# Moving the next block's queries between scores and values, and a block's first sums of exponentials by up to a unit, in a four-layer kernel on one core

## The chip, the cores and the metric

The kernel runs on one core of one Trainium2 chip. The metric is the device time of one execution in microseconds (us). The core has five engines that run side by side, each through its own instructions in order: PE (TensorE, products), DVE (VectorE), ACT (ScalarE, which does the exponentials), POOL (GpSimd) and SP (SyncE, which issues transfers). An engine waits for another one through semaphores.

## The reference, cut to what matters

The input `x` has 4 images of 128 channels and 64 x 64 pixels, so 4096 tokens of 128 channels per image. Four layers follow each other, and each adds its result to its input:

```
x = x + attention(group_norm(x))       # layer 0, self-attention over the 4096 tokens of an image
x = x + conv5x5(group_norm(x))         # layer 1
x = x + state_space(group_norm(x))     # layer 2, a scan over the 4096 tokens, both directions
x = x + conv3x3(group_norm(x))         # layer 3
```

The change lies in layer 0. Its core is

```
q, k, v = xt @ Wq.T + bq, xt @ Wk.T + bk, xt @ Wv.T + bv
attn = softmax((q @ k.T) * 128 ** -0.5)
out = attn @ v
```

## The kernel before, in words

**Images and stages.** An image goes through attention, the 5 x 5 convolution (`conv_pairs`), the preparation of the scan (`scan_prep`, `scan_operands`), the scan itself (`scan_core`) and, later, the last convolution. Layers 0 and 1 and the preparation of image b+1 are generators whose steps are put between the ticks of image b's scan. So image 0's attention stands alone, and the attention of images 1, 2 and 3 runs beside the scan of the image before. A `credit` decides how many steps go between two ticks: each step yields what it costs PE by the author's constants (`PRODUCT`, 0.86). The order of every engine's instructions is thus fixed when the program is built.

**Attention.** The weights of queries and keys are multiplied ahead of time into `wqk`, so the normalised image `xn` serves as keys. An image has 8 blocks of 512 tokens, and a block is worked off in 32 units of 128 keys; `u` counts all 256 units of an image, and `blk, j = divmod(u, 32)`. The pieces that matter:

- `queries(blk)`: a product `pr` of `wqk` and 512 columns of `xn` (L446), into PSUM bank "s"; then ACT copies it with a bias to `r` in SBUF (L448). It was called at `j == 17` for the next block, at the end of the unit.
- `scores(u)`: a product `sc` of 128 columns of `xn` and the block's `r` (L479), into bank "s" for even units and bank "s2" for odd ones; then ACT takes the exponential (L485) into slot `u % 8` of a ring in SBUF, called `exchange` in the profile.
- `values(w)`, two units behind: adds the product of `v` and ring slot `w` to `acc` (L491).
- `sums(w)`: sums of exponentials of four slots, as four products of 32 columns side by side, into `zp` (L513) in bank "z". In image 0 two other engines add them up in place of it (`side_sums`, L530 to L533). In images 1 to 3 a group of four is put on the list `due` with a first unit and a last one. `sums_due`, at the head of each unit, takes it in the first unit in which the scan has put its own products of 32 columns (`y`, L1272) before it, or else in the last one.
- At the end of a block `turn`, `invert`, `widen_out` and `settle` follow in units 1, 2, 4 and 5 after it. They use bank "z" too, and `settle` (L579, L580) is the last to read it, on DVE.

A float32 product of 512 columns is two passes on PE, so two rows in the profile. ACT's queue in images 1 to 3 also holds the scan's decays `da` (L1220) and copies of its last column (`last`, L1253). DVE runs the scan (`da`, `hc`, L1237 and L1240), POOL the products `db` (L1227) and part of the weighting (`hc`, L1258).

The whole program stands twice in the build; the second copy, with row maxima taken off, runs only where the sums leave a safe range.

Of the kernel before, what the change touches and what calls it, by code (L numbers as in the profile page):

```python
# [45 lines left out]
PRODUCT, HOP, SLOT, PACE, ENDPACE, AHEAD = 0.86, 1.7, 0.7, 2.8, 1.5, 4  # L46
# [6 lines left out]
def conv_preact_kernel(  # L53
# [26 lines left out]
    NM = L // MM  # L80
# [13 lines left out]
    def bank(tag, name):  # L94
        return pools.get(tag, ps).tile([P, MM], F32, tag=tag, name=name)
# [205 lines left out]
    NRING = 8  # L301
# [132 lines left out]
    def attention(b, xs, xn, v, st, safe, loads):  # L434
# [6 lines left out]
        def after(u, n, f, *args):  # L441
            later.setdefault(u + n, []).append((f, args))

        def queries(blk):
            pr = bank("s", f"pr_{b}_{blk}")
            nc.tensor.matmul(pr, wqk, xn[:, bass.ts(blk, MM)], start=True, stop=True)  # L446
            rq[blk] = pools["bg"].tile([P, MM], F32, tag="r", name=f"r_{b}_{blk}")
            nc.scalar.activation(rq[blk], pr, AF.Identity, bias=bqk)  # L448

        def row_max(blk):  # L450

            part = small.tile([P, TPM, NM], F32, tag="part", name=f"part_{b}_{blk}")
            for t in range(TPM):
                for k in range(NM):
                    pp = bank("s", f"pmax_{b}_{blk}_{t}_{k}")
                    nc.tensor.matmul(
                        pp, rq[blk][:, bass.ts(t, P)], xn[:, bass.ts(k, MM)],
                        start=True, stop=True,
                    )
                    nc.vector.tensor_reduce(part[:, t, k : k + 1], pp, AX.X, ALU.max)  # L460
            m = small.tile([P, TPM], F32, tag="rmax", name=f"rmax_{b}_{blk}")
            nc.vector.tensor_reduce(m, part, AX.X, ALU.max)
            pb = bank("s", f"pmb_{b}_{blk}")
            spread(pb, m)
            mb[blk] = pools["bg"].tile([P, MM], F32, tag="w", bufs=4, name=f"mb_{b}_{blk}")
            nc.scalar.copy(mb[blk], pb)
# [9 lines left out]
        def scores(u):  # L476
            blk, j = divmod(u, NJT)
            sc = bank(("s", "s2")[u % 2], f"sc_{b}_{u}")
            nc.tensor.matmul(sc, xn[:, bass.ts(j, P)], rq[blk], start=True, stop=True)  # L479
            pt = ring[:, u % NRING, :]  # L480
            if safe:
                nc.vector.tensor_tensor(pt, sc, mb[blk], ALU.subtract)
                nc.scalar.activation(pt, pt, AF.Exp)
            else:
                nc.scalar.activation(pt, sc, AF.Exp)  # L485

        def values(u):
            blk, j = divmod(u, NJT)
            if j == 0:
                acc[blk] = bank("a", f"acc_{b}_{blk}")  # L490
            nc.tensor.matmul(  # L491
                acc[blk], v[:, j, :], ring[:, u % NRING, :], start=j == 0, stop=j == NJT - 1
            )
# [3 lines left out]
        due = []  # L497

        def sums_due(u):
            beside = "collected" in ready  # L500
            ready.discard("collected")
            if due and due[0][1] <= u and (beside or u >= due[0][2]):
                sums(due.pop(0)[0])
                return PRODUCT
            return 0.0

        def sums(u):

            blk, j = divmod(u, NJT)
            if j == 3:  # L510
                zp[blk] = bank("z", f"zp_{b}_{blk}")
            for g in range(4):
                nc.tensor.matmul(  # L513
                    zp[blk][g * 32 : (g + 1) * 32, :], ones[:, :32],
                    ring[:, (u - 3 + g) % NRING, :], start=j == 3, stop=j == NJT - 1,
                    tile_position=(0, g * 32), skip_group_check=True,
                )
# [7 lines left out]
        def side_sums(u):  # L525
            blk, j = divmod(u, NJT)
            eng, e = (nc.vector, nc.gpsimd)[j % 2], "dp"[j % 2]
            if j < 2:
                sides[blk, e] = fill.tile([P, MM], F32, tag=f"side{e}", name=f"side{e}_{blk}")
                eng.tensor_copy(sides[blk, e], ring[:, u % NRING, :])  # L530
            else:
                s = sides[blk, e]
                eng.tensor_tensor(s, s, ring[:, u % NRING, :], ALU.add)  # L533

        def evict_sums(blk):
            zs = None
            if not fill:
                zs = pools["bg"].tile([P, MM], F32, tag="zs", bufs=1, name=f"zs_{b}_{blk}")
                nc.scalar.copy(zs, zp.pop(blk))
            state[blk] = None, zs  # L540

        def evict(blk):
            raw = pools["bg"].tile([P, MM], F32, tag="raw", bufs=1, name=f"raw_{b}_{blk}")
            nc.scalar.copy(raw, acc.pop(blk))
            state[blk] = raw, state[blk][1]
# [44 lines left out]
        for u in range(N):  # L590
            blk, j = divmod(u, NJT)
            cost = sums_due(u)
            if safe and j == 0:
                row_max(blk)
            scores(u)
            cost += PRODUCT
            w = u - 2
            if w >= 0:
                if w < N - HELD:
                    values(w)  # L600
                    cost += PRODUCT
                d = w % NJT
                if fill:
                    side_sums(w)
                elif d == NJT - 1:
                    sums(w)
                    cost += PRODUCT
                elif d % 4 == 3:
                    due.append((w, u + (2 if d == 3 else 1), u + NRING - 5))
                if d == NJT - 1:  # L610
                    evict_sums(blk - 1)
                    evict(blk - 1)
                    for n, f in ((1, turn), (2, invert), (4, widen_out), (5, settle)):
                        after(u, n, f, blk - 1)
            if j == 17 and blk + 1 < NM:
                queries(blk + 1)
                cost += PRODUCT
            for f, args in later.pop(u, ()):
                f(*args)
                cost += PRODUCT if f in (turn, widen_out) else 0.0  # L620
            next(loads, None)
            yield cost or HOP
        for w in (N - 2, N - 1) if fill else ():
            side_sums(w)
        blk = NM - 1
# [718 lines left out]
    def program(safe):  # L1344
# [24 lines left out]
        def front(b, xn, v):  # L1369

            xs = large(b + 1, f"xs_{b}")[:, :L]
            st = Sums(f"e{b}")
            yield from attention(b, xs, xn, v, st, safe, load(xs, b))
            st2 = Sums(f"s{b}")

            yield from conv_pairs(b, xs, f"A{b % 2}", st, st2, b > 0 or safe)
            if b + 1 == B:
                nc.sync.dma_start(m3, main_w)

            def mat(name):  # L1380
                return dram.tile([NCH, P, CH], F32, tag=name, name=f"{name}_{b}")

            mats4[b] = (
                [mat("bm"), mat("cm")], mat("dd"), mat("dxd"), mat("xcd"),
                dram.tile([P, L], F32, tag="xsd", bufs=B, name=f"xsd_{b}"),
            )
            ynds[b] = dram.tile([NM, P, MM], F32, tag="ynd", bufs=B, name=f"ynd_{b}")
            operands = yield from scan_prep(b, xs, st2, mats4[b])
            if b + 1 < B:
                return (yield from both(operands, start(b + 1, 10)))  # L1390
            yield from operands
            last_weights()
# [215 lines left out]
```

## Time and profile before

| | us |
|---|---|
| median of 3 runs | 4472.4 |
| lowest and highest of them | 4471.19, 4475.15 |
| the profiled execution's own time | 4469.3 |
| its span, first to last instruction | 4467.5 |
| PE busy in it | 3980.8 (89%) |
| DVE busy | 3726.3 (83%) |
| POOL busy | 3638.1 (81%) |
| ACT busy | 2399.7 (54%) |

The clock that PE was granted is 0.942 of full speed in the mean over the span. Scores (L479) take PE 1084.4 us and values (L491) 1048.4, the largest two of its groups; the scan's `y` 654.6, the sums 201.6. A busy time says how full an engine is and not whether it sets the pace; for that one cuts the span into stages and reads, stage by stage, which engine waits for which. In the trace, "idle before" a row, in brackets, names the engine and line that ended the wait. Where two rows of ACT end close together, a wait of PE for the first may be put down to the second (`last` in place of `r`).

### The profile page before, as it was taken

Reading aid. Unit: us, or ns where it says so; the run is one execution under the profiler, and the core shown is the slowest. Engines: PE = TensorE matmul, PEld = TensorE weight load, DVE = VectorE, ACT = ScalarE, POOL = GpSimd, SP = SyncE. Lnnn points to the kernel's source line nnn. Section 1 sums busy time; section 2 is a strip of 40 time slices with the busy share of each in tenths; the row PEclk is TensorE's granted clock in tenths of the full one; section 3 lists DMA queues with packets and bytes.
Section 4 is the critical chain, followed back from the end, with each engine's and each line's share of the span. In section 5 each row is a group of like instructions: output and inputs, shape, how many; then the busy total and the mean of one; then the engine's idle time right before and its main releaser. Section 6 shows DMA issues by size and latency. Waiting matters only on the chain. (4 is left out here: it accounts for less than half of the span.)

```text
span 4467.5 us, 43584 instructions
## 1 busy us (share of the span) xinstructions
PE 3980.8 (89%) x13480; PEld 1470.8 (33%) x13480; DVE 3726.3 (83%) x3703; ACT 2399.7 (54%) x4425; POOL 3638.1 (81%) x1728
## 2 busy tenths in 40 slices
PE   8999997999999979999999989999999758576776
PEld 4444433333333323333333333333333112121222
DVE  4712217999999989999999899999999899999995
ACT  3333217666665476666664576666654744444542
POOL 3433207999999978999999889999999889999995
PEclk9999999999999999999999999999999879787888
DMA  1000016544454565454545565455445666656562
GB/s 63 9 1 1 0 51 227 177 171 169 171 186 158 176 224 202 172 177 172 175 152 171 202 236 177 163 177 179 170 163 177 220 221 204 227 202 230 185 229 79
DMA packets 210002, 719.86 MB, mean 161 GB/s; under 512 B 24800, under 2 KB 25696, under 8 KB 209632
## 3 DMA queue, kind: packets, MB, share of 16 engines
q1 hardware_dynamic: 208160, 716.26, 45.9%
q8 instruction: 108, 1.77, 0.2%
q14 instruction: 134, 1.10, 0.1%
q10 hardware_dynamic: 1600, 0.73, 0.1%
HBM read 649.07 MB, written 67.83 MB: 160 GB/s over the span
## 5 line engine op out<-in xcount | busy, mean ns | idle before, releaser
L1227 POOL TENSOR_TENSOR db<-dx,br 128x1024 f32<-128x1024 f32 x1024 | 2399.9, 2365 | 231.1 <-DMA br<-bm 55.0
L1220 ACT ACTIVATE da<-de,a_neg 128x512 f32<-128x512 f32 (+1 forms) x1796 | 1342.9, 751 | 665.3 <-DVE da L1237 378.0
L479 PE MATMUL sc<-r,x 128*128 128x512 f32 x2048 | 1084.4, 612 | 16.0 <-ACT r L448 11.5
L491 PE MATMUL acc<-exchange,v 128*128 128x512 f32 x2048 | 1048.4, 594 | 1.7
L1258 POOL TENSOR_TENSOR hc<-hc,cr 128x1024 f32<-128x1024 f32 x401 | 947.7, 2363 | 19.3 <-ACT last L1253 16.5
L485 ACT ACTIVATE exchange<-sc 128x512 f32<-128x512 f32 x1024 | 604.7, 591 | 590.5 <-PE sc L479 583.8
L1272 PE MATMUL y<-hc,sel 128*32 128x512 f32 x4096 | 654.6, 652 | 270.6 <-POOL hc L1258 261.1
L1240 DVE TENSOR_TENSOR hc<-da,cr 128x512 f32<-128x512 f32 (+1 forms) x1078 | 835.5, 775 | 69.7 <-issue 0.9
L1237 DVE TENSOR_TENSOR_SCAN da<-da,last,db 128x512 f32<-128x512 f32 (+1 forms) x464 | 728.2, 1569 | 14.4 <-POOL db L1227 10.7
L1237 DVE TENSOR_TENSOR_SCAN da<-da,da,db 128x512 f32<-128x512 f32 x455 | 585.7, 1287 | 22.6 <-ACT da L1220 21.8
L479 PEld LDWEIGHTS sc<-r,x 128*128 128x128 f32 x2048 | 360.1, 190 | 607.8 <-issue 380.4
L491 PEld LDWEIGHTS acc<-exchange,v 128*128 128x128 f32 x2048 | 387.0, 190 | 496.7 <-issue 478.4
L1237 DVE TENSOR_TENSOR_SCAN hc<-da,last,db 128x512 f32<-128x512 f32 (+1 forms) x304 | 455.7, 1499 | 3.7 <-POOL db L1227 1.9
L1237 DVE TENSOR_TENSOR_SCAN hc<-da,hc,db 128x512 f32<-128x512 f32 x317 | 406.7, 1283 | 41.4 <-ACT da L1220 11.4
L533 POOL TENSOR_TENSOR sidep<-sidep,exchange 128x512 f32<-128x512 f32 x120 | 170.5, 1421 | 279.1 <-ACT exchange L485 276.9
L1272 PEld LDWEIGHTS y<-hc,sel 128*32 128x32 f32 x4096 | 92.9, 111 | 727.6 <-POOL hc L1258 350.9
L533 DVE TENSOR_TENSOR sided<-sided,exchange 128x512 f32<-128x512 f32 x120 | 96.1, 801 | 227.4 <-ACT exchange L485 226.1
L936 PE MATMUL pe<-df,cw 128*128 128x512 f32 x560 | 253.3, 597 | 0.0
L1237 DVE TENSOR_TENSOR_SCAN da<-da,db 128x512 f32<-128x512 f32 (+1 forms) x159 | 236.0, 1484 | 13.0 <-ACT da L1220 8.6
L678 PE MATMUL pcm<-xpm,cw 128*128 128x512 f32 x432 | 227.0, 670 | 15.5 <-ACT xpm L384 15.5
L513 PE MATMUL zp<-exchange,ones 128*32 128x512 f32 x1536 | 201.6, 596 | 8.0 <-DVE xs L580 7.9
L1253 ACT COPY last<-da 128x1 f32<-128x1 f32 x474 | 73.9, 156 | 249.4 <-DVE hc L1240 247.4
(239 smaller groups left out, 2829.8 us busy)
## 6 DMA issues: line engine op xcount, KB each, us to landing
br<-bm SPq DMA_DIRECT2D x512, 512.0 KB, 5.2
cr<-cm SPq DMA_DIRECT2D x512, 512.0 KB, 3.9
de<-dd SPq DMA_DIRECT2D x64, 512.0 KB, 4.7
dx<-dxd SPq DMA_DIRECT2D x64, 512.0 KB, 6.2
x<-in_x_dram SPq DMA_DIRECT2D x16, 512.0 KB, 5.1
xs<-in_x_dram SPq DMA_DIRECT2D x16, 512.0 KB, 5.6
xsd<-xs SPq DMA_DIRECT2D x16, 512.0 KB, 6.7
xcd<-xc SPq DMA_DIRECT2D x16, 512.0 KB, 2.8
```

Source lines behind the costliest of these rows:

```text
L479: nc.tensor.matmul(sc, xn[:, bass.ts(j, P)], rq[blk], start=True, stop=True)
L485: nc.scalar.activation(pt, sc, AF.Exp)
L491: nc.tensor.matmul(acc[blk], v[:, j, :], ring[:, u % NRING, :], start=j == 0, stop=j == NJT - 1)
L533: eng.tensor_tensor(s, s, ring[:, u % NRING, :], ALU.add)
L678: nc.tensor.matmul(acc.rearrange("p (r w) -> p r w", w=W), weights[:, t, :], xp[:, y : y + RPM, dx : dx + W], start=t == 0, stop=t == k * ...
L936: nc.tensor.matmul(flat(acc), cw[:, w * K5 + dx, :] if w < HSUM else more[:, w - HSUM, dx, :], view(r, dx), start=k == 1, stop=k == total ...
L1220: nc.scalar.activation(da, rep["de", b, c, d, g][:, bass.ts(h, size)], AF.Exp, scale=a_neg[:, at(i)])
L1227: nc.gpsimd.tensor_tensor(dbs[i], rep["dx", b, c, d, g], rows["b", b, c, d, q], ALU.mult)
L1237: nc.vector.tensor_tensor_scan(h, da, db[:, cut], before, ALU.mult, ALU.add)
L1240: nc.vector.tensor_tensor(hc[:, cut], h, rows["c", b, c, d, q][:, cut], ALU.mult)
L1258: nc.gpsimd.tensor_tensor(hcs[i], hcs[i], rows["c", b, c, d, q], ALU.mult)
L1272: nc.tensor.matmul(y[r : r + SG, :], sel, hcs[i - KG + 1 + gg][:, bass.ts(h, MM)], start=q == 0, stop=False, tile_position=(0, r), skip_gr ...
```

## The change

Two things are changed in the loop over units. The call of `queries(blk + 1)` at `j == 17` moves from the end of the unit to the place between `scores(u)` and `values(u - 2)`. And the first group of sums of a block (`d == 3`, that is slots 0 to 3 of the block) is due from unit `u + 3` on in place of `u + 2`; its last unit, `u + NRING - 5`, is `u + 3` as before.

```diff
             scores(u)
             cost += PRODUCT
+
+            if j == 17 and blk + 1 < NM:
+                queries(blk + 1)
+                cost += PRODUCT
             w = u - 2
             if w >= 0:
                 if w < N - HELD:
...
                     sums(w)
                     cost += PRODUCT
                 elif d % 4 == 3:
-                    due.append((w, u + (2 if d == 3 else 1), u + NRING - 5))
+                    due.append((w, u + (3 if d == 3 else 1), u + NRING - 5))
                 if d == NJT - 1:
                     evict_sums(blk - 1)
                     evict(blk - 1)
                     for n, f in ((1, turn), (2, invert), (4, widen_out), (5, settle)):
                         after(u, n, f, blk - 1)
-            if j == 17 and blk + 1 < NM:
-                queries(blk + 1)
-                cost += PRODUCT
             for f, args in later.pop(u, ()):
                 f(*args)
```

## The prediction

> **What bounds the kernel now.** I read the page's slices first: TensorE (PE) is the fullest engine up to about 3500 us, then VectorE (DVE) and GpSimd (POOL). "Busy" doesn't say who sets the pace, so I cut the span by stage with the view of windows (us from the span's start; busy time of each engine). The first row is image 0's attention, the next three are the attention of images 1, 2 and 3 beside the scan of the image before, the last is the scan's end.
>
> ```profile
> core 0: us, PE busy (x) PEld busy (x) DVE busy (x) ACT busy (x) POOL busy (x), PEclk, DMA share, GB/s
> 28.00:420.00 392.00, 386.10 (x1005) 178.16 (x1006) 163.95 (x203) 139.69 (x239) 147.42 (x105) 1.00 0.01 3
> 740.00:1340.00 600.00, 592.93 (x2245) 217.76 (x2243) 564.62 (x580) 385.33 (x793) 558.01 (x241) 1.00 0.51 179
> 1686.00:2280.00 594.00, 588.06 (x2230) 216.08 (x2234) 560.23 (x576) 380.70 (x786) 549.39 (x237) 1.00 0.51 177
> 2630.00:3280.00 650.00, 641.49 (x2444) 234.31 (x2444) 613.77 (x632) 416.56 (x854) 601.83 (x262) 1.00 0.52 178
> 3560.00:4387.00 827.00, 557.06 (x1640) 153.81 (x1640) 797.16 (x471) 384.81 (x613) 785.66 (x357) 0.79 0.60 213
> ```
>
> The reader is to see that PE is 98.5 to 99% busy in all four attentions, alone in the first (DVE 42%), with DVE at 94% close behind in the others, and that the last 827 us belong to DVE. Next, what PE waits for: in image 0 (28 to 420 us) one row is all there is; from 740 to 3300 us the three rows below are those that fall inside the attention loops.
>
> ```profile
> PE sc L479 <- ACT r L448: 6.0, 8, 0.8
> ```
> ```profile
> PE zp L513 <- DVE xs L580: 7.9, 12, 1.0
> ...
> PE sc L479 <- ACT r L448: 4.7, 6, 0.8
> PE sc L479 <- ACT last L1253: 4.5, 7, 0.8
> ```
>
> So the only stall of PE in image 0 is the scores that follow a block's queries. One such place in the timeline (start, duration, engine, operation):
>
> ```profile
> 56.79 1.02 PE L479 MATMUL sc<-r,x 128*128 128x512 f32 x2
> ...
> 57.65 1.02 PE L491 MATMUL acc<-exchange,v 128*128 128x512 f32 x2
> ...
> 57.91 0.60 ACT L485 ACTIVATE exchange<-sc 128x512 f32<-128x512 f32 x1 [1.18 <-PE sc L479]
> ...
> 58.51 1.02 PE L446 MATMUL pr<-x,wqk 128*128 128x512 f32 x2
> ...
> 59.57 0.69 ACT L448 ACTIVATE r<-pr,bqk 128x512 f32<-128x512 f32 x1 [1.06 <-PE pr L446]
> ...
> 60.31 1.13 PE L479 MATMUL sc<-r,x 128*128 128x512 f32 x2 [0.78 <-ACT r L448]
> ```
>
> A product is two passes and costs PE 0.86 us from start to start (56.79, 57.65, 58.51). Scores of unit 18 and queries share the PSUM bank "s", so the scores wait until ScalarE (ACT) has read `pr`: they start 1.80 us after the queries, not 0.86. 0.94 us is lost.
>
> **What the Trainium skill says.** "PSUM — Partial Sum Buffer", section "PSUM bank collisions raise a hardware error": a bank must be guarded as a whole between a matmul that writes and an engine that reads. The wait above is of that kind. "TensorE: Matmul & The Clock Gate", section "Architectural detail": PE can pull weight loads ahead of running matmuls, ACT is strictly first in, first out. Both show here: weights of a pass load during the pass before, and `r` never starts before the exponentials issued ahead of it. "TensorEngine Tiling (Array Packing)", section "Key Properties": a change of tiling mode drains PE. The trace prices it: acc to y (32 columns) takes 0.52 us from pass to pass where 0.43 is usual.
>
> **The change, part by part.** The instruction order of the changed kernel against that of before is the same on DVE, ACT, POOL and SP. (Three pairs of waits of `da` swap their source on ACT; I cost them nothing, as the same buffers are read.) Nothing is added, and no DMA moves. On PE 28 queries pass one `values` product each, and one group of sums passes one unit.
>
> *Queries.* Now scores(17), queries, values(15), scores(18). `values` needs nothing from `r`, so it runs while ACT reads `pr`. Queries start 0.86 us earlier (57.65), `r` 0.86 earlier if ACT is free: exp(17) ends at 58.51, the queries at 58.67, so it is. `r` then starts at 58.71, scores at 59.45 in place of 60.31; PE gets there at 59.37. Gain 0.86 of the 0.94. Image 0 has 7 of them (8 rows in the wait less the first block's): **7 x 0.86 = 6.0 us**. PE sets image 0's path alone (DVE, POOL and ACT are busy under 42% there), and what PE waits for from 420 to 740 us, such as 8.9 us for the group norm after the attention, hangs on the attention's end: all of it reaches the end.
>
> Images 1 to 3 have 21. In 11, products `y` of the scan, with or without sums, follow the queries before the next scores and cover the read already: gain 0. Ten stall 0.78 in the trace (13 in the two rows above, less the first scores at 1686 us and two others, at 1337 and 2985). For each I took the later of exp(17)'s end and the earlier queries' end as the new start of `r`. At 862, 1810, 2132, 2674, 2835 and 2996 us ACT is free: 0.86 each, 5.16. At 1971 exp(17) ends at 1969.00, `r` started at 1969.79: 0.79. At 1024:
>
> ```profile
> 1022.08 0.58 ACT L485 ACTIVATE exchange<-sc 128x512 f32<-128x512 f32 x1
> ...
> 1023.02 0.69 ACT L448 ACTIVATE r<-pr,bqk 128x512 f32<-128x512 f32 x1 [0.37 <-PE pr L446]
> ...
> 1023.76 1.13 PE L479 MATMUL sc<-r,x 128*128 128x512 f32 x2 [0.78 <-ACT r L448]
> ```
>
> exp(17) ends at 1022.66 behind two `da`, so only the 0.37 of idle ahead of `r` goes; the same at 1187. At 3157 `r` stood right behind exp(17): 0. **Sum 5.16 + 0.79 + 0.74 = 6.7 us.**
>
> Does that reach the end? PE gains 1.6, 2.5 and 2.6 us per attention. What could keep it is DVE, but DVE itself waits there for `da` of ACT, which stands behind exponentials that wait for PE. In 2630 to 3280:
>
> ```profile
> DVE da L1237 <- ACT da L1220: 9.1, 10, 2.1
> DVE hc L1237 <- ACT da L1220: 4.2, 9, 1.5
> ```
>
> 13.3 us of room for 2.6 (9.2 for 1.6 and 13.7 for 2.5 in the others), and after eight of the nine places DVE's own waits add up to more than the gain within some 42 us (after 1187 within 120). POOL waits too (558 to 602 us busy of 594 to 650). I take the gain in full; if DVE kept all of it, it would be 0.
>
> *The wait that moves.* Queries need bank "s" free of exp(16). They now ask 0.86 us earlier. In the trace exp(16) ends 0.92 us ahead of that in image 0, and 0.12 to 2.1 ahead in 20 of the 21 others; at 3074 us it is 0.30 late. Behind the waiting queries stands `values`, then `y` or scores. Cost **0.3 us**; at most 0.86 each, since before the change `values` filled exactly that time. At a stalling place it only eats the gain.
>
> *First sums.* The due time u+3 is now the deadline itself. 23 of the 24 blocks with sums on PE took them at the deadline before; only image 2's block 0 moves (1701 us), from behind `y` to behind `values`. That makes PE change its tiling once more: y-to-scores 0.52 and values-to-sums 0.52 in place of 0.43 each: **0.2 us** lost. Bounds 0 and 0.5, no gain, as PE did not wait at 1701 us (a changed wait on `xs`, 0.66 us on average in the row above, can't come in here: block 0 has no block before it). The 12 waits of `zp` on DVE stay.
>
> **Sum**: 6.0 + 6.7 - 0.3 - 0.2 = **12.2 us**. The profiled execution took 4469.3 us (span 4467.5), 3.1 below the median of 4472.4; made against it, 4457.1. Against the median: **4460.2 us**. A measurement of this kernel can tell about 0.2%, 8.9 us, from no change.
>
> **Rivals.**
> 1. *DVE keeps what the scan stretches give.* For: DVE is at 94% and its small gaps between dependent instructions fill much of the rest; PE waits 7.9 us for DVE's `xs`, and a faster PE waits there longer. Against: the 36 us of DVE's waits for `da`. Then image 0's 6.0 and up to half of 6.7 remain: -6 to -9, **4464 to 4466**, mostly under the 0.2%.
> 2. *More than counted.* `r` leaves ACT earlier in the 11 covered places too, and `da` with it; if half of them gave 0.86, -17: **4455**.
> 3. *Slower: exp(16) is late.* If ACT, with `da` ahead in its queue, ends exp(16) later relative to a PE that has gained, each of the 21 scan queries stops PE by up to 0.86, 18 us less the 6.0 of image 0: at most +12, **4484**. It decides where exp(16) slips by over 0.7 us in nearly all 21; today one is late. Little speaks for it.
> 4. *The second half does nothing*: it holds in 23 of 24 blocks, and is in the sum.
>
> **Chances.** All passes or nearly all (-10 to -14): 0.62. Rival 1: 0.27, a third of it past 8.9 us. Rival 2: 0.07. Rival 3: 0.04, of which half past +8.9; the rest about nothing. So faster 0.78, same 0.20, slower 0.02. The range takes rival 1 whole and most of 2, with some 2 us of a median's spread (4471.2 to 4475.2 before): 4455 to 4468.
>
> **What would show it.** PE's wait `sc` on `r` in 28 to 420 us falls from 6.0 to near 1 (the first block's 0.6 and small rests); in the scan stretches ten waits of 0.78 shrink to three (0.4, 0.4, 0.8). The first scan product of image 0 comes 6 us earlier. DVE's waits for `da` fall by some us. Wrong if: waits of `pr` on `exchange` appear (rival 3), `zp` on `xs` grows by as much as `sc` loses (rival 1), or the stretch 28 to 420 isn't shorter by 6.

## The result, and the profile after

The changed kernel takes 4457.05 us (median of 8 runs, 4453.91 to 4462.91), the kernel before 4471.33 (8 runs, 4467.22 to 4475.15). The ratio is 0.9968, with a 95% interval of 0.9958 to 0.9978: 14.3 us less, where the prediction had 12.2. On another occasion (last experiment) the ratio was 0.9972 (0.9963 to 0.9980), 12.6 us between the medians. The profiled execution took 4455.06 us, its span 4453.2.

PE's waits in image 0's attention (view of waits; engine and line, what it waited for, us in total, times, longest), changed kernel, 28 to 414 us:

```profile
PE sc L479 <- ACT r L448: 0.6, 1, 0.6
```

Before it was 6.0 us in 8 places. What is left is the first block, whose scores have nothing ahead of them. The same view from 734 to 3290 us:

```profile
PE zp L513 <- DVE xs L580: 7.9, 12, 1.0
...
PE sc L479 <- ACT r L448: 1.8, 3, 0.8
...
PE sc L479 <- ACT last L1254: 1.0, 3, 0.5
...
PE pr L446 <- ACT exchange L485: 0.2, 1, 0.2
```

The two rows of scores fell from 9.2 to 2.8 us. The waits of `zp` on `xs` are the 12 and the 7.9 us of before: the second half of the change did nothing to them. The last row is new: one place where the queries, now earlier, wait for exp(16).

The place that the prediction took apart, in the changed kernel (timeline: start, duration, engine, operation):

```profile
56.73 1.02 PE L479 MATMUL sc<-r,x 128*128 128x512 f32 x2
...
57.59 1.02 PE L446 MATMUL pr<-x,wqk 128*128 128x512 f32 x2
...
58.45 1.02 PE L491 MATMUL acc<-exchange,v 128*128 128x512 f32 x2
...
58.65 0.69 ACT L448 ACTIVATE r<-pr,bqk 128x512 f32<-128x512 f32 x1 [0.20 <-PE pr L446]
...
59.39 0.30 PEld L479 LDWEIGHTS sc<-r,x 128*128 128x128 f32 x2 [0.75 <-ACT r L448]
59.39 1.12 PE L479 MATMUL sc<-r,x 128*128 128x512 f32 x2
```

`values` (acc) runs while ACT reads `pr`. Scores(17) to scores(18) takes 2.66 us in place of 3.52: 0.86 less, as predicted, and PE's idle 0.78 is gone. A small rest of the wait is left: the weights of scores(18) still load late. Three products one after the other would take 2.58, so scores(18) starts 0.08 us late, and its two passes take 1.12 us where 1.02 is usual, another 0.10. Before, that row was 1.13 long too, so a block lost 0.94 + 0.10 = 1.04 us; now it loses 0.18.

The stages, in the same windows as before, shifted with the work (busy time of each engine):

```profile
28.00:414.00 386.00, 385.60 (x1005) 178.15 (x1006) 164.31 (x203) 139.69 (x239) 147.34 (x105) 1.00 0.01 3
732.50:1329.20 596.70, 591.60 (x2245) 217.18 (x2243) 563.76 (x580) 384.55 (x793) 557.70 (x241) 1.00 0.52 180
1675.50:2268.10 592.60, 588.55 (x2230) 215.69 (x2234) 559.32 (x575) 380.98 (x786) 549.22 (x237) 1.00 0.51 177
2616.00:3264.80 648.80, 642.47 (x2444) 234.91 (x2444) 613.51 (x632) 416.40 (x855) 602.01 (x262) 1.00 0.51 178
3545.50:4372.50 827.00, 555.52 (x1640) 153.76 (x1640) 798.15 (x470) 385.86 (x614) 788.21 (x357) 0.79 0.60 214
```

The same instructions stand in each row (PE x1005, x2245, x2230, x2444, x1640), the four attention rows are shorter, by 6.0, 3.3, 1.4 and 1.2 us, and the end of the scan is 827 us as before. So 11.9 of the 14.3 us by which the two spans differ lie in the attentions, and 2.4 between the stages; more on these below.

A sharper gauge is the loop itself, from the start of an image's first scores to that of its last (unit 255), read from the trace of each kernel:

| us, from first to last scores | image 0 | image 1 | image 2 | image 3 |
|---|---|---|---|---|
| before | 468.72 | 638.11 | 636.27 | 634.31 |
| changed | 462.71 | 634.94 | 635.02 | 632.75 |
| changed, another execution | 462.71 | 634.17 | 633.78 | 633.93 |

Image 0 repeats to 0.01 us, the others to some 1 us between the two executions of the changed kernel.

### The profile page after: what moved, and what is told of

It reads as the page before. It is cut to its first block, busy times and chain, and to the rows that moved or that the text cites. A ratio compares the mean times of both kernels' runs of the same rounds, so it can differ in the third digit from the quotient of the medians.

```text
span 4453.2 us, 43584 instructions
## 1 busy us (share of the span) xinstructions
PE 3977.4 (89%) x13480; PEld 1470.5 (33%) x13480; DVE 3725.2 (84%) x3703; ACT 2399.5 (54%) x4425; POOL 3638.9 (82%) x1728
## 5 line engine op out<-in xcount | busy, mean ns | idle before, releaser
L1238 DVE TENSOR_TENSOR_SCAN da<-da,last,db 128x512 f32<-128x512 f32 (+1 forms) x464 | 728.0, 1569 | 15.3 <-POOL db L1228 13.4
```

Of the source, the lines that this page charges most:

```text
L1238: nc.vector.tensor_tensor_scan(h, da, db[:, cut], before, ALU.mult, ALU.add)
```

## The experiments

The comparisons gave ratios to the kernel before; medians stand beside them. "Loop" is the gauge above.

**Queries alone.** The queries moved, the first sums as they were:

```diff
-                    due.append((w, u + (3 if d == 3 else 1), u + NRING - 5))
+                    due.append((w, u + (2 if d == 3 else 1), u + NRING - 5))
```

> Queries moved as in the change, first sums as before. My theory (PE sets the pace in all four attentions, the moved product covers ACT's read of pr): 6.0 us from image 0 and 6.7 - 0.3 from the scan stretches, 12.4 us less than before, so as fast as the changed kernel within 0.2 us of working. Rival that the sums carry a part of the gain: less than the changed kernel's 14.3 by several us.

4457.8 us against 4471.5, ratio 0.9974 (0.9964 to 0.9984), which alone leaves 7 to 16 us open. Loops 462.71, 634.61, 633.42, 632.41: those of the changed kernel, to 1.6 us. So the gain is here, and the next experiment finds none in the sums.

**Sums alone.** The queries back at the end of the unit, the sums due at `u + 3`:

```diff
-                    due.append((w, u + (2 if d == 3 else 1), u + NRING - 5))
+                    due.append((w, u + (3 if d == 3 else 1), u + NRING - 5))
```

> First sums due at u+3, queries where they were. My theory: one group of sums of 24 moves, 0.2 us slower at most, PE's waits of zp on xs stay at 12 and 7.9 us. Rival that the sums carry the gain: several us faster, with fewer waits of zp.

4471.06 us against 4471.5, ratio 1.0000 (0.9992 to 1.0009), and PE's waits of `zp` on `xs` are again 7.9 us in 12 places. The 0.2 us of an added change of tiling is far below what this comparison tells; a gain of over 3.6 us, as the rival had it, is ruled out.

**Image 0 alone, and images 1 to 3 alone.**

```diff
-            if j == 17 and blk + 1 < NM:
+            if j == 17 and blk + 1 < NM and b == 0:
                 queries(blk + 1)
```

with the rest of the images calling it at the end of the unit; in the second kernel the condition is `b > 0`. The sums are as before in both.

> Queries moved in image 0 alone. My theory: scan products begin 6.0 us earlier and the whole is 6.0 us shorter, but for what PE's granted clock does after 500 us. Rival (the gain of image 0 is kept by a later wait): nothing at the end, although image 0 is shorter by 6.0.

> Queries moved in images 1 to 3 alone. My theory: ten stalls of PE shrink to three, 6.7 - 0.3 = 6.4 us shorter at the end, nothing before 780 us. Rival (DVE, busy at 94%, keeps what PE gains): 0 to 3 us shorter, and PE's waits of zp on xs or of y on hc grow by what the scores lose.

Image 0 alone: 4464.95 us against 4471.5, ratio 0.9986 (0.9979 to 0.9992), that is 6.3 us by the ratio (3.6 to 9.4) for an expected 6.0. Loops 462.71, 635.41, 636.38, 634.28. Images 1 to 3 alone: 4463.88, ratio 0.9984 (0.9977 to 0.9990), 7.2 us for an expected 6.4, and the loops of images 1 to 3 are shorter than before's, that of image 0 is not: 468.72, 635.74, 633.10, 632.61. The two parts add up to the whole within their intervals. PE's waits in the second one, 735 to 3300 us:

```profile
PE zp L513 <- DVE xs L580: 7.9, 12, 1.0
...
PE sc L479 <- ACT r L448: 2.7, 4, 0.8
PE y L1275 <- POOL hc L1261: 1.5, 2, 0.8
PE sc L479 <- ACT last L1256: 0.8, 2, 0.5
```

Before, in the same stretch, the two rows of scores were 5.5 and 4.5 us, `zp` 7.9 and `y` 2.3. So `zp` and `y` did not take over what the scores lost; DVE and POOL did not keep it. The interval of this half is 4.5 to 10.3 us, so the 0 to 3 of the rival are outside it.

**A dose the other way.** With the queries moved and the sums as before, in images 1 to 3 each block's queries but the first are multiplied twice, the first product thrown away:

```diff
-            nc.tensor.matmul(pr, wqk, xn[:, bass.ts(blk, MM)], start=True, stop=True)
+            for _ in range(2 if b > 0 and blk > 0 else 1):
+                nc.tensor.matmul(pr, wqk, xn[:, bass.ts(blk, MM)], start=True, stop=True)
```

> Queries moved, sums as before; in images 1 to 3 each block's queries but the first are multiplied twice into the same bank (the first product is thrown away), 21 products or 18.1 us of PE more in the scan stretches. My theory (PE sets the pace there): 18 us slower than with queries moved alone, so about 5 us slower than before. Rival (DVE sets the pace, PE has room): 0 to 6 us slower than with queries moved alone, still well below before.

4475.11 us, ratio to the kernel before 1.0008 (1.0001 to 1.0014), so 17.3 us above queries alone by the medians and 15.2 by the ratios (some 10 to 20, with both intervals), for 18.1 us of products. Loops 462.71, 639.69, 640.36, 636.88: those of images 1 to 3 are together 15.3 us above the means of the kernels with the move (given below). DVE's waits for decays, from 2640 to 3280 us of this kernel:

```profile
DVE da L1238 <- ACT da L1221: 10.2, 12, 2.1
DVE hc L1238 <- ACT da L1221: 5.9, 12, 1.6
```

and from 2616 to 3264.8 us of the changed kernel:

```profile
DVE da L1238 <- ACT da L1221: 8.6, 10, 2.1
DVE hc L1238 <- ACT da L1221: 3.7, 10, 1.0
```

DVE waits 16.1 us where PE is given more, 13.3 in the kernel before, 12.3 where PE is given less. In images 1 and 2 the order is the same: 12.7, 9.2, 7.8 and 14.9, 13.7, 11.2. So DVE follows PE: at 94% busy it was the second engine, not the one that set the pace.

**Queries ahead of scores(17).** They ask for bank "s" one product earlier still; their call at the end of the unit goes, as in the change:

```diff
+            if j == 17 and blk + 1 < NM:
+                queries(blk + 1)
+                cost += PRODUCT
             scores(u)
```

> Queries ahead of scores(17), so that they ask for bank s 0.86 us earlier still; sums as before. My theory: image 0 gains 7 x (0.94 - 0.06) = 6.2 us; in the scan stretches the stall of scores goes wholly (10 x 0.94 less a little, ACT does r ahead of exp(17)), but queries now wait for exp(16): by the profile of before exp(16) ends too late in 14 of 21 places, 4.7 us in all. So about 10 to 11 us faster than before, 2 us less than queries after scores, and PE's wait of pr on exchange grows from 0.2 us to some 4 to 5. Rival (the wait for exp(16) costs nothing): 15 us faster than before. Rival (it costs much more once ACT is pressed): under 6.

4458.24 us against 4471.41, ratio 0.9974 (0.9964 to 0.9985): no different from queries after scores. The rival of under 6 us is just outside the interval (6.7 to 16.1 us); that of 15 is inside it, and what speaks against it is the new wait below. The loop of image 0 is 462.08, so 0.95 of the 1.04 us a block is won there (6.64 us; queries did not wait). In the scan stretches the new wait came, at somewhat under the price:

```profile
PE pr L446 <- ACT last L1253: 8.9, 2, 5.6
PE pr L446 <- ACT exchange L485: 3.1, 5, 1.0
```

3.1 us where 4.7 were worked out (the first row is the first queries of an image, as before). Loops 636.37, 635.71 and 633.29 are each longer than with queries alone (634.61, 633.42, 632.41): what image 0 wins seems to be given back, though single executions scatter by as much.

**Image 0's queries into another bank**, with the queries moved and the sums as before:

```diff
-            pr = bank("s", f"pr_{b}_{blk}")
+            pr = bank("z" if fill and blk else "s", f"pr_{b}_{blk}")
```

> Queries moved as in the change, sums as before, and in image 0 the queries' product goes to bank z, so that the next scores need not wait for the read of it. My theory: what is left of the stall in image 0 is 0.18 us a block (scores 0.51 and 0.53 us after the pass before, in place of 0.43), so 1.3 us less than with queries moved alone, 13.7 below before; image 0 is 7.3 us shorter. Rival (the rest has another cause, such as the weight load): no difference.

4456.45 us, ratio 0.9970 (0.9958 to 0.9982); the total can't tell 1.3 us. The loop of image 0 can: 461.78, so 0.93 less, and scores(17) to scores(18) is 2.58 us, three products and nothing else, at all seven blocks. The two passes of scores(18) are back at 1.02 us as well, so 0.18 us a block is won, 1.3 in seven; elsewhere in that loop one unit took 0.38 longer (3.88 in place of 3.50), which makes the 0.93. So the rest of the stall was the bank; the late weight load came with the wait for it and went with it. The Trainium skill, "Perfetto Trace Analysis", section "Matmuls", advises independent products to go through different PSUM banks so that the read-out of one runs beside the next; the trace agrees: another bank was worth 0.18 us a block here, with a product already in between. At the old place the wait for the bank cost 1.04, but another bank was not tried there.

**Settling a unit earlier**, with the queries moved and the sums as before:

```diff
-                    for n, f in ((1, turn), (2, invert), (4, widen_out), (5, settle)):
+                    for n, f in ((1, turn), (2, invert), (3, widen_out), (4, settle)):
```

> Queries moved, sums as before, and widen_out and settle a unit earlier (3 and 4 units after the block), so that bank z is read out before the first sums are due. My theory: PE's 12 waits of zp on xs (7.9 us) vanish; up to 7.9 us less than with queries moved alone. Rival (a wait moves, it does not go): pzb waits for zr, or ACT's square of xs, now a unit earlier in its queue, holds the exponentials behind it; then no gain or a loss of some us in each image.

4456.18 us, ratio 0.9968 (0.9956 to 0.9980). PE's waits from 735 to 3310 us have no row of `zp` on `xs` any more, and in its place

```profile
PE pzb L471 <- DVE zr L567: 7.2, 8, 2.4
```

where it was 3.9 in 2. Of 7.9 us gone 3.3 came back here; loops 462.71, 635.13, 632.58, 631.26. The total is 1.6 us under queries alone, or 2.7 by the ratios, and the intervals overlap, so a gain is not shown.

**Both of the last two together (their two diffs), and the changed kernel once more on the same chip.**

> Queries moved, image 0's queries in bank z, widen_out and settle a unit earlier, sums as before. My theory: the two effects add where PE sets the pace: 0.9 to 1.3 us from image 0, and of the 7.9 us of zp's waits what pzb's new ones (3.3 us) leave, so 3 to 5 us less than the changed kernel. Rival (the second only moves waits about): within 1.5 us of the changed kernel.

> The changed kernel once more on the same chip as the version above: 12 to 14 us below before. My theory expects 12.2, and its loop of image 0 at 462.7 us from the first scores to the last, as in its first profile; if the 14.3 of the first comparison holds more than chance, it comes out at 14 again.

Both together: 4454.7 us against 4472.29, ratio 0.9963 (0.9949 to 0.9977), loops 461.40, 635.76, 632.51, 632.00. The changed kernel on the same chip: 4459.69, ratio 0.9972 (0.9963 to 0.9980), loops 462.71, 634.17, 633.78, 633.93. The 5.0 us between the medians (4.0 by the ratios), for an expected 3 to 5, point to a better version, but the intervals overlap. Of it 1.3 are shown, in image 0's loop.

## Why the prediction was right, point by point

**Image 0, 6.0 us.** The loop fell by 6.01 in every kernel that moved the queries there to this place and left them in their bank, and the comparison of image 0 alone says 6.3. That PE alone sets the path there was right.

**Scan stretches, 6.7 less 0.3.** For the loops of images 1 to 3 I take the means of the three kernels without the move there (before, sums alone, image 0 alone: 637.03, 636.72, 634.23) and of the four with it (the changed kernel twice, queries alone, images 1 to 3 alone: 634.87, 633.83, 632.93). The differences are 2.2, 2.9 and 1.3, in all 6.4. (With the kernel of the other bank as a fifth, 6.2.) By image the prediction had 1.6, 2.5 and 2.6 before its two deductions, and single executions scatter by a us or two. So the sum is shown to some 2 us and the split is not; that it meets the 6.4 to the digit is luck. The reading place by place also held: where ACT was busy with exp(17), a rest of the stall stayed.

```profile
1010.41 1.02 PE L446 MATMUL pr<-x,wqk 128*128 128x512 f32 x2
1011.27 1.02 PE L491 MATMUL acc<-exchange,v 128*128 128x512 f32 x2
1012.58 1.12 PE L479 MATMUL sc<-r,x 128*128 128x512 f32 x2 [0.29 <-ACT r L448]
```

That is the place at 1024 us of before (0.78 to 0.29, where 0.4 was expected); 0.30 is left at its twin and 0.76 at 3142 us, where nothing was expected to go. The six counted in full show no wait any more. The one at 1971 us of before, sized at 0.79, kept 0.19 here, and nothing in the repeat or with queries alone. Taken from the start of the queries to that of the scores, the ten places gave 0.86 six times, then 0.59, 0.49, 0.48 and 0.02, in all 6.7 us: the sum predicted, with misses of 0.1 to 0.2 at three places that cancel.

**The wait that moves, 0.3.** One place, 0.18 us:

```profile
3058.28 1.12 PE L446 MATMUL pr<-x,wqk 128*128 128x512 f32 x2 [0.18 <-ACT exchange L485]
```

It is the one that the trace of before had shown as late. The rival built on it (exp(16) late nearly everywhere) failed: even with the queries a product earlier still, these waits came to 3.1 us in 5 of 21 places.

**First sums, 0.2.** Not told from nothing by the time; waits unchanged.

**Rival 1, DVE keeps the gain.** Refuted by the half with images 1 to 3 alone, and by the dose, of which 15 to 17 of 18.1 us reached the end by the medians, the ratios and the loops. That DVE keeps a small part is not excluded. DVE's waits for `da` fell from the 36 us of before to 31, as the prediction had it ("some us").

**Rival 2, more than counted.** Its 17 us lie inside the interval of the total. The loops speak against it: it would take some 4.7 us more from images 1 to 3 than the 6.4 found.

**Where 14.3 and 12.2 differ.** Two us lie inside the interval (10 to 19 us), and the repeat gave 12.6. The loops account for some 12.4. Outside them, one stretch was shorter in the profiled execution: the products that spread the last block's reciprocals, right after image 0's loop. Before, in the changed kernel, and in the changed kernel's repeat:

```profile
504.40 1.91 PE L471 MATMUL pzb<-ident,zr 128*128 128x128 f32 x8
```
```profile
497.67 1.05 PE L471 MATMUL pzb<-ident,zr 128*128 128x128 f32 x8
```
```profile
500.26 1.72 PE L471 MATMUL pzb<-ident,zr 128*128 128x128 f32 x8
```

The granted clock over these rows was 0.50, 1.00 and 0.59 of full speed. From image 0's last scores to the end of these products took 8.7 us before, 7.2 in the changed kernel and 8.85 in its repeat, so the change is not what wins these 1.5 us. With queries alone the reduced clock fell on the products just ahead (0.51 over the first row, 0.99 over the second), and the stretch took 8.9:

```profile
496.03 3.66 PE L491 MATMUL acc<-exchange,v 128*128 128x512 f32 x4
499.51 1.07 PE L471 MATMUL pzb<-ident,zr 128*128 128x128 f32 x8
```

The scan's first product tells the same: counted from image 0's first scores, it came 7.6 us earlier in the profiled execution of the changed kernel and 6.3 in the repeat, where 6 were predicted. So part of the difference in the profiled execution is chance, read from the trace and not tried; the other executions left no trace to read it from.

## What to carry to other kernels

Where a product's bank must be read out before the next product on that bank, put a product that needs neither between them: the read's latency then costs little (here 0.18 us in place of 1.04), and what it wins can be worked out as the smaller of that product's time and the idle time, place by place. Check first what else stands in the reader's queue, since behind other work only its idle time can be won. Which of two nearly full engines sets the pace is told by which one waits for the other, and a dose of extra work on it shows it better than its busy share.

## What the runs showed of the hardware

The loop of image 0, 256 units over 460 us, repeats to 0.01 us between executions and between kernels that issue the same products there (468.72 in three kernels, 462.71 in six executions of five), while loops that run beside the scan move by up to 2.7 us for the same order (image 1: 638.11, 637.57, 635.41). Eight short products took 1.91 us at a granted clock of 0.50 and 1.05 at 1.00, and one and the same kernel met 1.00 in one execution and 0.59 in the next. So a gain of a us is measured in a stage that repeats, not in the total.
